# Two wave loads of the recurrence requested ahead of images 1 to 3

## The chip, the cores and the metric

The kernel runs on one core of one Trainium2 chip. The metric is the device time of one execution in microseconds (us), as the median of several runs. Profiles come from one further execution, which is recorded by the hardware profiler.

## The reference

Four images of 56 x 56 pixels with 128 channels pass through four layers:

- a neighbourhood attention (7 x 7 windows, four heads) with an MLP behind it,
- a recurrence of 16 steps with gates (three matrix products per pixel), whose complex coefficients come from Fourier transforms of two 7 x 7 kernels per channel,
- a softmax attention over all pixels and a mixture of eight experts, of which each pixel uses two,
- an attention by distances and a layer of 64 experts that choose their tokens.

What the change touches belongs to the second layer's coefficients:

```
A_f = fft2(pad(A_real + 1j * A_imag))        # 64 channels, 56 x 56
Ar, Ai = A_f.real, A_f.imag
mag = sqrt(Ar ** 2 + Ai ** 2 + 1e-08)
scale = 0.95 * sigmoid(mag) / (mag + 1e-08)
Ar, Ai = Ar * scale, Ai * scale              # and B_f without a scale
for _ in range(16):
    h_r, h_i = (fg_r * (Ar * h_r - Ai * h_i) + inp_r,
                fg_i * (Ar * h_i + Ai * h_r) + inp_i)
```

## The kernel before

The images stay in SBUF from start to end as `x[0]` to `x[3]`, 112 partitions (two image rows) by 28 tiles by 128 channels, and each layer adds its result to them. The first layer runs over 28 stripes of eight image rows, seven per image. `PERIOD` is a list, written by hand, of the steps of one round with their lags: round `i` computes the scores of stripe `i+1`, the sums of stripe `i`, the MLP of stripes `i-1` and `i-2`, and so on. The order of the instructions on TensorE, VectorE and ScalarE is exactly this order (`tc.manual_schedule`). Each of these engines works in order, so an instruction that waits holds up all behind it.

**The recurrence's transforms.** `Recurrence.transforms` works out the Fourier transforms as matrix products with a table of cosines and sines (`waves`, 113 rows: cosines in rows 0 to 48, sines in rows 64 to 112). It cuts the 1568 columns of half an image into eight portions of n = 196 columns. A portion is four steps: `products` (L1070: eight products with `taps` into two `f_ps`, copies into `fa` and `fb`, squares), `squared`, `magnitudes` and `scaled`. They are laid into the rounds of the first layer by `WAVES_AT`, one portion for each round, from round 1 on; `products` stands in each round behind the sums of the stripe (L713, L719).

Each `products` begins with the request of its part of the waves (L1073), 113 partitions by 2 by 196 numbers of 4 bytes. The part goes into two rows of `parts`, 0 and 1 for even portions, 4 and 5 for odd ones (`places`), so the request for portion 2 waits until TensorE is through with portion 0.

**The requests.** All DMA requests of this stretch are made by SyncE, in the order of the program text. In `neighbourhood_of_safe_scores` this order is: the bands and weights of the first layer; stripes 3 to 6 of image 0; then, from `transforms`, `taps` (113 rows), `gates_w`, `gates_b`, `group` and `late` (L1042 to L1046); then images 1 to 3, one request of 1568 KB each (L158); and then, as the rounds reach them, the eight parts of the waves:

```
        env.fetch(0, range(3, NG))
        plan = work(ps1, NG + 1)
        for b in range(1, B):
            env.fetch(b)
```

`work` is what calls `transforms`. The rounds come after these lines, and with them the requests of L1073.

**Who reads images 1 to 3 first.** The step `ahead` (L560, `bn_stats` on VectorE) takes the statistics of coming stripes. The step "statistics" calls it up to three times in each round, and it starts out ahead: stripes 7 and 8, the first two of image 1, come in round 0. Behind them on VectorE stand, in round 0, the copy of `b_vT` (L813) and the late constants of the projection, for which TensorE waits at L817, then the quotient (L727 to L732) and the bands (L675). Image 2 is first read in round 3.

Of the kernel before, what the change touches and what calls it, by code (L numbers as in the profile page):

```python
# [32 lines left out]
WAVES = 64 + K7 * K7  # L33
# [96 lines left out]
class Env:  # L130
# [41 lines left out]
    def load(self, pool, name, src):  # L172
        t = pool.tile(list(src.shape), F32, tag=name, name=name)
        self.nc.sync.dma_start(t, src)
        return t
# [826 lines left out]
class Recurrence:  # L1002
# [35 lines left out]
    def transforms(self, psum):  # L1038


        nc, ins, n = self.env.nc, self.env.ins, HALF // 8
        nc.sync.dma_start(self.taps, ins["taps"])  # L1042
        nc.sync.dma_start(self.gates_w, ins["gates_w"])
        nc.sync.dma_start(self.gates_b, ins["gates_b"])
        nc.sync.dma_start(self.group, ins["groups"])
        nc.sync.dma_start(self.late, ins["L0_conv_b_fc2"].unsqueeze(1))  # L1046

        def constants():
            nc.vector.tensor_scalar(
                self.gates_b[:, 0, :], self.gates_b[:, 0, :], 2.0, 0.5, ALU.add, ALU.mult  # L1050
            )
            nc.vector.tensor_scalar(
                self.gates_b[:, 1, :], self.gates_b[:, 1, :], 0.5, None, ALU.mult
            )
            nc.vector.tensor_scalar(self.group, self.group, 1.0 / (TOK * GC), None, ALU.mult)
            nc.vector.tensor_scalar(
                self.taps[64:WAVES, :, 1, :], self.taps[64:WAVES, :, 1, :], -1.0, None, ALU.mult
            )
            if not self.is_late:
                nc.vector.memset(self.late, 0.0)  # L1060
                nc.vector.memset(self.gates_b[:, 3, :], 0.0)

        def places(c0):

            at = 4 * (c0 // n % 2)
            return self.parts[:WAVES, at : at + 2, :n], *(
                self.parts[:, at + i, :n] for i in (2, 3)
            )

        def products(c0):  # L1070
            cols = slice(c0, c0 + n)
            waves, mag, _ = places(c0)
            nc.sync.dma_start(  # L1073
                waves, ins["waves"].rearrange("w (k t) -> w k t", k=2)[:, :, cols]
            )
            for i, out in enumerate((self.fa[:, 0:2], self.fb)):
                f_ps = psum.tile([128, 2, n], F32, tag="one", name="f_ps")
                for j in range(2):
                    for k, side in enumerate(self.SIDES):
                        nc.tensor.matmul(  # L1080
                            f_ps[side, j, :], self.taps[:, i, j, :], waves[:, k, :],
                            start=True, stop=True,
                        )
                nc.scalar.copy(out[:, :, cols], f_ps)
            nc.scalar.activation(self.fa2[:, cols], self.fa[:, 0, cols], AF.Square)
            nc.scalar.activation(mag, self.fa[:, 1, cols], AF.Square)

        def squared(c0):
            fa2, mag = self.fa2[:, c0 : c0 + n], places(c0)[1]
            nc.vector.tensor_tensor(fa2, fa2, mag, ALU.add)  # L1090


        def magnitudes(c0):
            fa2 = self.fa2[:, c0 : c0 + n]
            _, mag, gain = places(c0)
            nc.scalar.activation(mag, fa2, AF.Sqrt, bias=self.tiny)
            nc.scalar.activation(gain, mag, AF.Tanh, scale=0.5)

        def scaled(c0):
            fa, fa2 = self.fa[:, 0:2, c0 : c0 + n], self.fa2[:, c0 : c0 + n]  # L1100
            _, mag, gain = places(c0)
            nc.vector.tensor_scalar(mag, mag, 1e-8, 2.0 / 0.95, ALU.add, ALU.mult)
            nc.vector.reciprocal(mag, mag)
            nc.vector.scalar_tensor_tensor(gain, gain, 1.0, mag, ALU.add, ALU.mult)
            nc.vector.tensor_tensor(
                fa, fa, gain.unsqueeze(1).to_broadcast([128, 2, n]), ALU.mult
            )
            nc.vector.tensor_tensor(gain, gain, gain, ALU.mult)
            nc.vector.tensor_tensor(fa2, fa2, gain, ALU.mult)

        return constants, [
            [lambda c0=c0, step=step: step(c0) for step in (products, squared, magnitudes, scaled)]
            for c0 in range(0, HALF, n)
        ]
# [495 lines left out]
class Paced:  # L1610
# [6 lines left out]
    def step(self, share):  # L1617

        begun = set()
        while self.at < len(self.pieces):  # L1620
            piece = self.pieces[self.at]
            if share < 1 and (
                self.due[self.at] > self.total * share
                or getattr(piece, "apart", False) and getattr(piece, "list", None) in begun
            ):
                return
            piece()
            begun.add(getattr(piece, "list", None))
            self.at += 1
# [1386 lines left out]
```

## Time and profile before

| | us |
|---|---|
| median of 3 runs (lowest, highest) | 2504.63 (2502.03, 2505.33) |
| the profiled execution's own time | 2503.91 |
| its span, first to last instruction | 2502.0 |
| TensorE busy | 2386.4 (95%) |
| VectorE busy | 1841.4 (74%) |
| ScalarE busy | 1552.2 (62%) |
| GpSimd busy | 211.4 (8%) |

The span is shorter than the execution by what lies around the first and the last instruction. In the profile PE is TensorE's products and PEld its loading of weights, DVE is VectorE, ACT ScalarE, POOL GpSimd, SPq SyncE's queue of requests. A row of 40 digits cuts the span into slices of 62.6 us; the digit is the busy share in tenths. The mean clock that TensorE was granted is 0.97 of full speed. Line numbers are those of the kernel before.

### The profile page before, as it was taken

Reading aid. Unit: us, or ns where it says so; the run is one execution under the profiler, and the core shown is the slowest. Engines: PE = TensorE matmul, PEld = TensorE weight load, DVE = VectorE, ACT = ScalarE, POOL = GpSimd, SP = SyncE. Lnnn points to the kernel's source line nnn. Section 1 sums busy time; section 2 is a strip of 40 time slices with the busy share of each in tenths; the row PEclk is TensorE's granted clock in tenths of the full one; section 3 lists DMA queues with packets and bytes.
Section 4 is the critical chain, followed back from the end, with each engine's and each line's share of the span. In section 5 each row is a group of like instructions: output and inputs, shape, how many; then the busy total and the mean of one; then the engine's idle time right before and its main releaser. Section 6 shows DMA issues by size and latency. Waiting matters only on the chain.

```text
span 2502.0 us, 39490 instructions
## 1 busy us (share of the span) xinstructions
PE 2386.4 (95%) x14685; PEld 1294.7 (52%) x14685; DVE 1841.4 (74%) x5062; ACT 1552.2 (62%) x3343; POOL 211.4 (8%) x473
## 2 busy tenths in 40 slices
PE   6999999999999999999999999999999999996795
PEld 4777777775455555555544444445444434442334
DVE  5556899983997959799598687745888567777563
ACT  3899889875666646666422556484554765844681
POOL 4323354320000000000000000000000000000000
PEclk9999999999999999999999999999999998997688
DMA  6000000000000000000000000000000000002266
GB/s 141 13 10 2 2 2 2 2 2 9 1 1 1 1 1 1 1 1 1 12 1 1 1 1 1 1 1 1 1 1 1 1 1 1 1 1 109 76 256 205
DMA packets 39917, 53.95 MB, mean 22 GB/s; under 512 B 4104, under 2 KB 35443, under 8 KB 35620
## 3 DMA queue, kind: packets, MB, share of 16 engines
q1 hardware_dynamic: 39716, 51.34, 6.4%
q8 instruction: 118, 1.93, 0.3%
q14 instruction: 83, 0.68, 0.1%
HBM read 44.78 MB, written 6.42 MB: 20 GB/s over the span
## 4 chain that ended last, share of the span: by engine, by line
PE 67%; DVE 6%; ACT 2%; DMA 1%; issue 1%; SPq 0%; DVEq 0%; ACTq 0%
PE s_ps L2027 20%; PE o_ps L2110 20%; PE y_ps L1557 7%; PE d_ps L1825 4%; PE xT_ps L207 3%; PE g_ps L1196 2%; PE p_ps L2307 1%; PE l_ps L2266 1%; PE y_ps L2051 1%; PE q_ps L1789 1%; PE z_ps L2003 1%; PE l_ps L1522 1%; PE h_ps L2376 1%; DMA lot<-in_L_ffn_lots 1%; DVE x L2459 1%; PE o_ps L2405 1%
## 5 line engine op out<-in xcount | busy, mean ns | idle before, releaser
L2034 ACT ACTIVATE e<-s_ps 128x448 f32<-128x448 f32 x688 | 367.8, 543 | 514.8 <-PE s_ps L2027 510.2
L2027 PE MATMUL s_ps<-zT,xnT 128*128 128x448 f32 (+1 forms) x1400 | 649.1, 554 | 0.6 <-ACT e L2034 0.6
L2110 PE MATMUL o_ps<-e,keep 128*128 128x448 f32 (+1 forms) x1376 | 646.1, 552 | 0.0
L2110 PEld LDWEIGHTS o_ps<-e,keep 128*128 128x128 f32 (+1 forms) x1376 | 241.3, 190 | 214.9 <-issue 213.8
L2027 PEld LDWEIGHTS s_ps<-zT,xnT 128*128 128x128 f32 (+1 forms) x1400 | 240.2, 188 | 212.8 <-issue 190.9
L1837 ACT ACTIVATE d_ps<-d_ps,half 128x448 f32<-128x448 f32 (+1 forms) x384 | 232.2, 606 | 118.3 <-PE d_ps L1825 116.2
L1831 DVE TENSOR_REDUCE found<-d_ps 128x1 f32<-128x448 f32 x316 | 190.9, 619 | 72.0 <-PE d_ps L1825 69.7
L1557 PE MATMUL y_ps<-experts,xnT 128*112 128x512 f32 x448 | 215.5, 604 | 2.0 <-ACT d_ps L1837 1.7
L1562 DVE TENSOR_TENSOR gated<-y_ps,gate 112x512 f32<-112x512 f32 x224 | 151.5, 687 | 37.6 <-PE y_ps L1557 35.3
L1567 DVE TENSOR_TENSOR gated<-gated 112x512 f32<-112x512 f32 (+1 forms) x336 | 152.4, 462 | 3.0
L1825 PE MATMUL d_ps<-q_near,k_near 32*128 32x448 bf16 (+1 forms) x700 | 138.3, 373 | 9.4 <-ACT d_ps L1837 4.0
L207 PE MATMUL xT_ps<-ident,xn 112*128 112x112 f32 x672 | 118.4, 281 | 24.9 <-ACT xn L1657 16.9
L207 PEld LDWEIGHTS xT_ps<-ident,xn 112*128 112x128 f32 x672 | 79.7, 145 | 100.7 <-ACT xn L1657 52.1
L1557 PEld LDWEIGHTS y_ps<-experts,xnT 128*112 128x112 f32 x448 | 76.2, 178 | 97.6 <-issue 60.4
L1825 PEld LDWEIGHTS <-k_near 32*128 32x128 bf16 (+1 forms) x700 | 33.4, 92 | 167.1 <-issue 154.3
L675 DVE TENSOR_TENSOR e<-e,band 112x1792 f32<-112x1792 f32 (+3 forms) x56 | 100.0, 1788 | 15.4 <-ACT e L668 15.4
L780 PE MATMUL f_ps<-w_fc,h 128*112 128x128 f32 x896 | 104.8, 274 | 1.9 <-ACT h L771 1.6
L1657 ACT ACTIVATE xn<-x,g_off,g_rs 112x128 f32<-112x128 f32 x224 | 94.1, 484 | 19.3 <-DVE g_off L1647 9.0
L780 PEld LDWEIGHTS f_ps<-w_fc,h 128*112 128x112 f32 x896 | 99.8, 177 | 5.2 <-ACT h L771 4.8
L766 PE MATMUL h_ps<-zT,w_fc 128*128 128x448 f32 x224 | 88.9, 540 | 0.6 <-ACT zT L760 0.6
L668 ACT ACTIVATE e<-s_ps 112x1792 f32<-112x1792 f32 (+3 forms) x56 | 82.7, 1477 | 7.0 <-PE s_ps L659 4.0
L1201 ACT ACTIVATE parts<-g_ps,gates_b 128x224 f32<-128x224 f32 x168 | 65.8, 449 | 21.3 <-PE g_ps L1196 15.4
(404 smaller groups left out, 3935.7 us busy)
## 6 DMA issues: line engine op xcount, KB each, us to landing
lot<-in_L_ffn_lots SPq DMA_DIRECT2D x32, 1024.0 KB
out_x<-x SPq DMA_DIRECT2D x28, 224.0 KB
x<-in_x SPq DMA_DIRECT2D x3, 1568.0 KB
x<-in_x SPq DMA_DIRECT2D x7, 224.0 KB
parts<-in_waves SPq DMA_DIRECT2D x8, 173.0 KB
out<-found SPq DMA_DIRECT2D x64, 2.0 KB
w_fc<-in_L_conv_w_fc SPq DMA_DIRECT2D x2, 256.0 KB
experts<-in_L_ffn_expert_w SPq DMA_DIRECT2D x1, 512.0 KB
```

Of the source, the lines that this page charges most:

```text
L207: self.nc.tensor.transpose(ps[:, j * P : (j + 1) * P], xn[:, j, :], self.ident[:P, :P])
L675: nc.vector.tensor_tensor(es, es, bands[stripes[i][1] == 0][:n].rearrange("p h r c -> p h (r c)").unsqueeze(2) .to_broadcast([n, NH, m, 8 ...
L780: nc.tensor.matmul(f_ps[:, j, :], h[:, k, j * P : (j + 1) * P], w_fc2[:, k, :], start=(k == 0), stop=(k == 3),)
L1557: nc.tensor.matmul(y_ps, held["xnT"][g][:, j * P : (j + 1) * P], self.experts[:, 4 * i : 4 * i + 4, :], start=True, stop=True,)
L1562: nc.vector.tensor_tensor(gated[:, some, :], y_ps, gate[:, some].unsqueeze(2).to_broadcast([P, 4, C]), ALU.mult,)
L1567: nc.vector.tensor_tensor(gated[:, :n, :], gated[:, :n, :], gated[:, n : 2 * n, :], ALU.add)
L1825: nc.tensor.matmul(d, held["k"][part, 128 * c : 128 * c + n], held["q"][g][part, :], start=True, stop=True,)
L1831: nc.vector.tensor_reduce(self.found[:, self.most : self.most + 1], d, AX.X, ALU.max)
L1837: nc.scalar.activation(d, d, AF.Relu, bias=self.half[:n], accum_out=self.found[:n, self.sums : self.sums + 1],)
L2027: nc.tensor.matmul(s_ps[i * n : (i + 1) * n, :GW], self.xnT[:, at : at + n], zT, start=True, stop=True,)
L2034: nc.scalar.activation(e[:n], s_ps[:n, :GW], AF.Exp)
L2110: nc.tensor.matmul(sums[:, :GW], self.keep[:n, k, :], e[:n], start=(k == 0 and g - 1 not in pairs), stop=last,)
```

## The change

The function that asks for a part of the waves becomes a function of its own, `load`. `transforms` calls it for portions 0 and 1 right behind its other five requests, and `products` calls it for the other six only. As `transforms` runs before images 1 to 3 are requested, the two requests now stand ahead of those three in SyncE's queue. The places in `parts`, the sizes, and the order of the instructions on the other engines stay as they are.

```diff
         nc.sync.dma_start(self.late, ins["L0_conv_b_fc2"].unsqueeze(1))
 
+        def places(c0):
+
+            at = 4 * (c0 // n % 2)
+            return self.parts[:WAVES, at : at + 2, :n], *(
+                self.parts[:, at + i, :n] for i in (2, 3)
+            )
+
+        def load(c0):
+            nc.sync.dma_start(
+                places(c0)[0],
+                ins["waves"].rearrange("w (k t) -> w k t", k=2)[:, :, c0 : c0 + n],
+            )
+
+        early = range(0, 2 * n, n)
+        for c0 in early:
+            load(c0)
+
         def constants():
...
         def products(c0):
             cols = slice(c0, c0 + n)
             waves, mag, _ = places(c0)
-            nc.sync.dma_start(
-                waves, ins["waves"].rearrange("w (k t) -> w k t", k=2)[:, :, cols]
-            )
+            if c0 not in early:
+                load(c0)
```

## The prediction

> **What bounds the kernel now.** First the page, for which engine sets the time and where its row has holes; then who TensorE waits for in the first 85 us; then what the request queue and the DMA engines do there.
>
> ```profile
> PE 2386.4 (95%) x14685; PEld 1294.7 (52%) x14685; DVE 1841.4 (74%) x5062; ACT 1552.2 (62%) x3343; POOL 211.4 (8%) x473
> ...
> PE   6999999999999999999999999999999999996795
> ...
> x<-in_x SPq DMA_DIRECT2D x3, 1568.0 KB
> ...
> parts<-in_waves SPq DMA_DIRECT2D x8, 173.0 KB
> ```
>
> TensorE is busy for 95%, and its row is full from the second slice on. Between 85 and 122 us the waits name none of TensorE, so what is lost or won before about 85 us reaches the end unchanged. The first slice (6) is the only place that this change can touch. Who waits there (in total, times, longest):
>
> ```profile
> PE f_ps L1080 <- DMA parts<-in_waves: 5.4, 1, 5.4
> ...
> DVE st_all L560 <- DMA x<-in_x: 5.0, 1, 5.0
> ...
> PE bp_ps L817 <- DVE b_vT L813: 1.3, 1, 1.3
> ```
>
> Two DMA waits, not one: TensorE waits 5.4 us for wave load 0, and before that VectorE waits 5.0 us for image 1, with TensorE behind it. The order in time, from the timelines of SyncE, VectorE and TensorE (start, us, instruction, count, idle before it):
>
> ```profile
> 28.64 16.21 SPq L158 DMA_DIRECT2D x<-in_x  x3
> 44.90 21.90 SPq L1073 DMA_DIRECT2D parts<-in_waves  x3
> ...
> 42.88 1.65 DVE L560 BATCH_NORM_STATS2 st_all<-x 112x6 f32<-112x128 f32 x8 [4.98 <-DMA x<-in_x]
> 44.44 0.15 DVE L813 COPY b_vT<-bv_ps 128x1 f32<-128x1 f32 x1
> ...
> 44.64 0.46 PE L817 MATMUL bp_ps<-w_proj,b_vT 128*96 128x128 f32 x2 [1.32 <-DVE b_vT L813]
> ...
> 63.26 2.88 PE L1080 MATMUL f_ps<-parts,taps 113*64 113x196 f32 x16 [5.37 <-DMA parts<-in_waves]
> 66.07 3.33 PE L641 MATMUL v_ps<-w_qkv,xnT 128*112 128x128 f32 x14
> ...
> 84.69 1.55 PE L1080 MATMUL f_ps<-parts,taps 113*64 113x196 f32 x16
> 86.17 1.78 PE L641 MATMUL v_ps<-w_qkv,xnT 128*112 128x128 f32 x14
> ```
>
> Image 1 releases VectorE at 42.88; TensorE is ready for the first products at 63.26 − 5.37 = 57.9 and gets load 0 at 63.26. Last, what the DMA engines moved in these stretches (length, then busy us of PE, PEld, DVE, ACT, POOL, clock, DMA share, GB/s):
>
> ```profile
> 28.90:36.70 7.80, 6.14 (x72) 3.23 (x70) 3.16 (x2) 4.84 (x6) 7.25 (x18) 1.00 0.99 216
> 36.70:37.30 0.60, 0.60 (x29) 0.55 (x32) 0.60 (x3) 0.44 (x1) 0.60 (x1) 1.00 0.19 37
> ...
> 52.60:54.60 2.00, 2.00 (x5) 0.71 (x4) 1.94 (x6) 0.00 (x0) 0.00 (x0) 0.50 0.11 28
> 54.60:62.60 8.00, 3.29 (x113) 3.08 (x112) 5.49 (x21) 0.72 (x2) 2.52 (x9) 0.92 0.07 22
> ...
> 45.60:55.80 10.20, 9.44 (x73) 6.30 (x77) 9.76 (x25) 3.15 (x5) 0.20 (x2) 0.50 0.76 166
> ...
> 63.20:69.40 6.20, 6.14 (x34) 4.99 (x34) 0.36 (x1) 2.08 (x5) 0.00 (x0) 0.50 0.08 25
> ```
>
> These rows decide the case. An image uses all 16 DMA engines (share 0.99). A wave load uses one: share 0.07 is 1/16, and 22 GB/s for 8.0 us is 176 KB, one load of 113 x 2 x 196 x 4 B = 177 KB. So **a wave load is small, but holds one DMA engine for 8.0 us**. And that engine is one that the images use: in 52.6 to 54.6 a single engine finishes image 3 while the rest stand still, and load 0, long requested, starts only then. `taps`, also 113 rows, shows what such a load does to what comes behind it: it is requested ahead of the images, and the 1.6 MB of image 1 have passed by 36.7 (216 GB/s for 7.8 us is 1.7 MB), yet VectorE gets image 1 only at 42.88. The rest came late through one engine.
>
> **The change part by part.** Instructions and their order on TensorE, VectorE, ScalarE and GpSimd are the same in both kernels. On SyncE's queue two requests (0 and 1) of the eight at L1073 move past three, images 1 to 3. They write places in `parts` that nobody uses before, so no wait for an earlier reader comes with them. Images 2 and 3 now take over DMA semaphores last used by `taps` and the gate weights, which have landed long before; no cost.
>
> *Taken away:* TensorE's wait for load 0, 5.4 us. Load 0 would land near 43, load 1 near 51, both before 57.9. The next loads (2 and 3) are requested behind products 0 and 1 as before and have a period of 18.5 us (84.69 to 103.19); no cost.
>
> *The two issues themselves:* 2 x 0.63 us on SyncE (its usual time for one), beside all engines; the DMA engine is the longer price, so nothing is added for them.
>
> *Added:* image 1's share on that one engine stands behind two loads, 2 x 8.0 = 16.0 us. So does its release of VectorE: 42.88 becomes about 58.9. Two rules of the Trainium skill pull apart here. For the change speaks "DMA: Bandwidth & Descriptors", section "Rules for kernel authors": issue a DMA early and wait on it late. With only 346 KB more to pass at 216 GB/s it would make image 1 late by 1.6 us, and the sum would be negative. Against it speaks the same page's "Queues, rings and completion order": each DMA engine consumes its ring in order, and a transfer has landed only when every engine it uses has reported. Then the 16.0 us are due in full. The row of 52.60 to 54.60 is on the second rule's side, so I take 16.0. Lower bound: image 1's share of that engine is 98 KB, 4.6 us alone at 22 GB/s; by the trace's landing records the last small load ahead of it there landed at 34.70, so it used 8.2 us beside the other engines. Saving all of that gives 12.4. Upper bound: loads that run beside images are slower. At 216/16 = 13.5 GB/s each would take 13 us, 26 together; but in 36.70 to 37.30 the other engines soon stand still when one lags, so I go to 18 at most. Image 2 is first read near 101 us and image 3 later; image 3's last landing record stands at 55.1, so 16 us late both are still there by 71.2.
>
> *Who stands behind that wait:* VectorE is in order, so the `b_vT` copy, the projection's constants, the transposes and the bands wait with it; TensorE, also in order, stands at bp_ps, and ScalarE behind TensorE. From 42.88 to 54.1 VectorE has no gap, so nothing in that stretch takes up a delay. TensorE comes to the first products at 57.9 + 16.0 = 73.9, which is 10.6 us after 63.26.
>
> *Given back by the clock.* After today's 4.7 us hole the clock is at 0.50 (63.20 to 69.40). If TensorE comes to the products without a hole, that stretch runs as the next period does: products 2.88 to 1.55, values 3.33 to 1.78, queries 1.67 to 0.92, the 24 scores 1.48 to 0.86, transposes 0.89 to 0.60, in all 4.5 us. ScalarE, 9.15 busy of 10 us in 80 to 90, would then be late for the next products' copies by an estimated 0.5 us; I count 4.0. Today the clock is back at 1.00 by 55.8, 11.2 us after the restart at 44.64; a restart near 60.7 would have it back by 71.9, ahead of 73.9. The skill's "TensorE: Matmul & The Clock Gate", section "Part 1: The HAM clock gate", speaks against the change here: an idle window drops the clock to half, so a 16 us stall buys a new slow start, worth up to half of the 10.2 us that follow. But the row of 45.60 to 55.80 is already at 0.50 today and led by VectorE (9.76 of 10.20 busy), so I charge nothing more. Bounds for the clock's part: −4.5 to +1.
>
> Sum: 16.0 − 5.4 − 4.0 = **+6.6 us**. On the profiled execution's 2503.9 (span 2502.0 and 1.9 around it) this is 2510.5; the median of the runs stands 0.7 higher, so 2511.2.
>
> **The rivals.**
>
> *Forecast, 0.60:* as above; with a delay of 14 to 17.5, +4 to +8.5.
>
> *The clock does not come back, 0.16:* the longer stall leaves TensorE at half speed through the first products too. Then 16.0 − 5.4 = +10.6: 2515.2. For it: 11.2 us of slow restart in today's trace. Against: 2 us of margin in the sum above.
>
> *One load's worth, 0.14:* the two loads overlap, or the engine's share of image 1 gets through between them. Delay 8 to 12, sum −1.4 to +2.6: no change that can be measured. Against: 54.6 to 70.6 shows two loads one after the other at 22 to 24 GB/s.
>
> *Faster, 0.10:* the images do not stand behind the loads, because the moved loads use an engine whose image share is not the last to land. Image 1 is late by 1.6 us, 1.6 − 5.4 − 4.0 = −7.8: 2496.8. It decides when the delay is under 5.4 + 4.0 = 9.4 us. For it: TensorE's wait is real and the bytes few. Against: today's 42.88, six us after image 1's bytes had passed.
>
> **How the numbers follow.** A measurement of this kernel can tell about 0.2%, 5.0 us, from no change. The forecast case lies mostly above +5.0: of its 0.60 I put 0.48 in slower and 0.12 in same; with 0.16 for the slow clock and a little of the third case, slower has 0.65. Same has 0.25, faster 0.10. The range, 2505.5 to 2516, holds the forecast, the slow clock and the upper end of the third case; the faster case is left out.
>
> **What would show it right or wrong in the profile after.** VectorE's wait for the image at L560 near 58 to 59 us, some 21 us long instead of 5.0. TensorE's wait for `b_vT` 17 us instead of 1.3. No wait for the wave loads at L1080, first products near 74, second near 91.3 (84.69 + 6.6). A DMA share of 0.07 for much of 29 to 47. The clock at 1.00 through the first products. I am wrong if VectorE gets image 1 before 52 us, or if the second products start within 2 us of 84.69.

## The result and the profile after

| | before | changed |
|---|---|---|
| median of 20 runs each, us | 2504.57 | 2510.42 |
| profiled execution, us (its span) | 2503.91 (2502.0) | 2512.44 (2510.6) |
| first products at L1080 / L1089, us | 63.26 | 73.06 |
| second products, us | 84.69 | 93.18 |
| from there to the end of the span, us | 2417.3 | 2417.4 |

The ratio of the runs is 1.0024 (95% interval 1.0017 to 1.0031): slower by 5.9 us, between 4.3 and 7.8. One of the 20 runs of the changed kernel took 4767.54 us in a slow state that no profile shows; the ratio leaves it out, and without it the median is 2510.20. In the changed kernel the lines behind `transforms` have moved by 9 (L1080 is L1089, the requests of L1073 are L1056). The last row of the table says that in these two profiled executions whatever differs lies before the second products; the 2417 us behind them are the same. That they agree so closely is in part chance: in the other eleven profiles of this document the same stretch takes 2415.0 to 2422.5 us. So times are compared by the medians of the runs, and the profiles serve for the first 95 us.

Who waits between 42 and 75 us in the changed kernel, from its waits (in total, times, longest):

```profile
...
DVE st_all L560 <- DMA x<-in_x: 19.0, 1, 19.0
ACT xnT L603 <- PE xT_ps L207: 16.2, 1, 16.2
...
PE bp_ps L817 <- DVE b_vT L813: 15.3, 1, 15.3
```

TensorE's wait for the wave loads is gone from this list. VectorE's wait for image 1 has grown from 5.0 to 19.0 us, TensorE's wait behind it from 1.3 to 15.3. The times, from the timelines of SyncE, VectorE and TensorE:

```profile
28.23 8.51 SPq L1056 DMA_DIRECT2D parts<-in_waves  x2
36.79 23.93 SPq L158 DMA_DIRECT2D x<-in_x  x3
...
58.43 1.65 DVE L560 BATCH_NORM_STATS2 st_all<-x 112x6 f32<-112x128 f32 x8 [18.97 <-DMA x<-in_x]
60.00 0.14 DVE L813 COPY b_vT<-bv_ps 128x1 f32<-128x1 f32 x1
...
60.19 0.74 PE L817 MATMUL bp_ps<-w_proj,b_vT 128*96 128x128 f32 x2 [15.31 <-DVE b_vT L813]
...
73.06 1.55 PE L1089 MATMUL f_ps<-parts,taps 113*64 113x196 f32 x16
74.54 1.78 PE L641 MATMUL v_ps<-w_qkv,xnT 128*112 128x128 f32 x14
...
79.51 1.02 PE L622 MATMUL q_ps<-xnT,w_qkv 128*128 128x448 f32 x2 [1.67 <-ACT xnT L603]
...
93.18 1.55 PE L1089 MATMUL f_ps<-parts,taps 113*64 113x196 f32 x16
```

Image 1 now releases VectorE at 58.43, 15.6 us later than before. What the DMA engines did meanwhile (columns: length, busy us of PE, PEld, DVE, ACT, POOL, clock, DMA share, GB/s):

```profile
28.90:36.70 7.80, 6.14 (x80) 4.50 (x79) 2.02 (x1) 5.48 (x8) 7.34 (x21) 1.00 0.08 25
36.70:44.00 7.30, 7.30 (x165) 5.63 (x165) 2.34 (x5) 2.37 (x6) 6.50 (x20) 1.00 0.08 24
44.00:48.00 4.00, 0.87 (x8) 0.69 (x7) 0.00 (x0) 1.47 (x1) 1.37 (x3) 0.82 0.71 179
48.00:52.00 4.00, 0.00 (x0) 0.00 (x0) 0.00 (x0) 0.00 (x0) 0.00 (x0) 0.50 1.17 226
...
73.00:79.50 6.50, 4.84 (x74) 3.91 (x66) 3.58 (x11) 4.69 (x9) 2.96 (x7) 1.00 0.04 13
80.80:87.40 6.60, 6.60 (x44) 5.10 (x37) 3.14 (x6) 5.87 (x8) 0.67 (x1) 0.50 0.04 12
```

From 28.90 to 44.00 little more than one engine of sixteen works (0.08; one is 0.06). Before, 216 GB/s of image 1 moved in the first of these rows. The images did not only lose their share on the one engine: by the packet records none of their parts started before 45, when load 1 was well under way (41.3 to 50.2). The last two rows are the clock: full through the first products, then half for nearly 7 us.

### The profile page after: what moved, and what is told of

Same layout as the page of the kernel before. It is cut to its first block, busy times and chain, and to the rows that moved or that the text cites. A ratio compares the mean times of both kernels' runs of the same rounds, so it can differ in the third digit from the quotient of the medians.

```text
span 2510.6 us, 39486 instructions
## 1 busy us (share of the span) xinstructions
PE 2384.3 (95%) x14685; PEld 1294.6 (52%) x14685; DVE 1840.9 (73%) x5062; ACT 1552.0 (62%) x3343; POOL 211.2 (8%) x473
## 4 chain that ended last, share of the span: by engine, by line
## 5 line engine op out<-in xcount | busy, mean ns | idle before, releaser
L1834 PE MATMUL d_ps<-q_near,k_near 32*128 32x448 bf16 (+1 forms) x700 | 137.6, 369 | 10.2 <-ACT d_ps L1846 4.3
```

The source lines that it names most:

```text
L1834: nc.tensor.matmul(d, held["k"][part, 128 * c : 128 * c + n], held["q"][g][part, :], start=True, stop=True,)
```

## The experiments

All times are medians against the runs of the kernel before that were made with them (2504.57 to 2505.56 us). The column "released" is when image 1 releases VectorE in the profile (a line of L560 with a DMA wait in front of it; "no wait" where there is none).

| run | released | first products | second products | time, us | ratio (95% interval) |
|---|---|---|---|---|---|
| changed, again | 57.37 | 71.99 | 92.11 | +5.1 | 1.0019 (1.0011 to 1.0026) |
| load 0 alone early | 49.25 | 63.74 | 83.83 | −1.6 | 0.9990 (0.9981 to 0.9999) |
| loads behind image 1 | 39.98 | 53.79 | 73.94 | −11.4 | 0.9957 (0.9944 to 0.9971) |
| early, on 16 engines | 43.26 | 55.62 | 75.74 | −8.2 | 0.9967 (0.9955 to 0.9979) |
| image 1 read later | 58.25 | 53.92 | 70.88 | −9.6 | 0.9964 (0.9950 to 0.9977) |
| taps on 16 engines | no wait | 57.70 | 74.65 | −9.5 | 0.9959 (0.9946 to 0.9973) |
| early loads and taps on 16 | 40.05 | 53.80 | 73.94 | −9.1 | 0.9963 (0.9950 to 0.9975) |
| loads behind image 1, hole filled | 40.00 | 55.73 | 73.14 | −11.4 | 0.9951 (0.9937 to 0.9966) |
| all on 16, nothing moved | no wait | 55.99 | 76.13 | −10.8 | 0.9951 (0.9938 to 0.9965) |
| the same, hole filled | no wait | 55.77 | 73.19 | −14.6 | 0.9936 (0.9922 to 0.9950) |
| changed, hole filled | 56.81 | 71.27 | 88.69 | +1.3 | 1.0006 (0.9998 to 1.0015) |

**One load instead of two.**

```diff
-        early = range(0, 2 * n, n)
+        early = range(0, n, n)
```

> Only load 0 stands ahead of images 1 to 3; load 1 is requested with its products. Theory (a load of 113 rows holds one DMA engine for 8 us, and image 1's share on that engine queues behind it): image 1 releases VectorE one load earlier than with two, near 58.4 - 7.9 = 50.5 us; first products near 65, second between 82 and 85.3; the time within -2.6 to +0.6 us of the kernel before. Rival (any request ahead of the images makes SyncE's queue hand them on late, whatever engines it uses): about as late as with two loads, near 58. Rival (the images are late only by the bytes ahead of them): near 43.7, first products near 59, time -5 to -8 us.

VectorE's line for image 1 in this run:

```profile
49.25 1.64 DVE L560 BATCH_NORM_STATS2 st_all<-x 112x6 f32<-112x128 f32 x8 [9.40 <-DMA x<-in_x]
```

One load less, 8.1 to 9.2 us earlier (57.37 and 58.43 in the two profiles of the changed kernel). Both rivals (58 or 43.7) are out. The gain and the loss nearly cancel: −1.6 us. So the delay goes by the load, and a break-even lies between one load and two.

**The loads between image 1 and image 2.**

```diff
         for b in range(1, B):
             env.fetch(b)
+            if b == 1:
+                work.requests()
```

`work.requests` calls `load` for the two early portions; the lines that take these calls out of `transforms` and hand them on are left out here.

> Loads 0 and 1 are requested between image 1 and image 2. Theory: image 1 releases VectorE at 42.9 as in the kernel before, the loads take the one engine from there on and land near 51 and 59, images 2 and 3 are 16 us late, which nobody meets before about 100 us. First products near 57.9 without a hole, second near 75 (clock at full speed throughout) to 78; time -6.5 to -10 us. Rival (the move costs because the two loads and the images share bandwidth, or because of the two issues themselves): no better than the changed kernel, +6 us. Rival (the first products wait for something else once the loads are there): no gain against the kernel before.

VectorE and TensorE in this run:

```profile
39.98 1.64 DVE L560 BATCH_NORM_STATS2 st_all<-x 112x6 f32<-112x128 f32 x8 [2.40 <-DMA x<-in_x]
...
53.79 1.55 PE L1090 MATMUL f_ps<-parts,taps 113*64 113x196 f32 x16
```

At the first products this is 4.1 us better than expected (57.9). Image 1 releases VectorE 2.9 us sooner than in the kernel before: its late share took 5.8 us and not 8.2 by the landing records, probably because no other image runs beside it. TensorE is at bp_ps 1.4 us sooner (43.25), and from there to the first products it takes 10.5 instead of 13.3 us: in the kernel before the clock was at half for some 10 us of that way (45.60 to 55.80), here only from 44.8 to 48.2. TensorE's wait for the loads is gone as in the changed kernel, and so is the stall. The idea of the change was sound; image 1 is what the two loads must not stand in front of.

**The same place, but sixteen engines.**

```diff
-            nc.sync.dma_start(
-                places(c0)[0],
-                ins["waves"].rearrange("w (k t) -> w k t", k=2)[:, :, c0 : c0 + n],
-            )
+            src = ins["waves"].rearrange("w (k t) -> w k t", k=2)[:, :, c0 : c0 + n]
+            for rows in (slice(0, 112), slice(112, WAVES)) if c0 in early else (slice(0, WAVES),):
+                nc.sync.dma_start(places(c0)[0][rows], src[rows])
```

> As the changed kernel, but each of the two early loads is requested as 112 rows and 1 row, so that it spreads over 16 DMA engines. Same bytes, same place in the queue, two requests more. Theory (the one engine is the price): image 1 is late by about 1.5 us only, VectorE released near 44; first products near 59, second between 76 and 79; time -5.5 to -8.5 us. Rival (bytes or requests ahead of the images are the price): VectorE released near 58 as in the changed kernel, time +6 us or more.

```profile
43.26 1.64 DVE L560 BATCH_NORM_STATS2 st_all<-x 112x6 f32<-112x128 f32 x8 [3.89 <-DMA x<-in_x]
```

The same bytes in the same place, with two requests more, take the delay away: 43.26 against 58.43, and −8.2 us against +5.9. The one engine, and so the number of rows, 113, was the price; the bytes and the place were not. The Trainium skill has the rule for it ("DMA: Bandwidth & Descriptors", section "Why a DMA increments its semaphore by 16 and not by 1"): a transfer runs on the largest number of engines up to 16 that divides the slowest dimension of both sides. 112 gives 16, the prime 113 gives 1. This case agrees: the share is 0.07 to 0.08 with 113 rows, and by the landing records the request of 112 rows reports from 16 engines, that of 113 rows from one.

**Image 1 read one round later.** The transfers are those of the changed kernel:

```diff
-                "statistics": lambda i: ahead_to(i + NG + 3),
+                "statistics": lambda i: ahead_to(NG - 1 if i <= 1 else i + NG + 3),
```

> As the changed kernel, but VectorE reads image 1 one round later: its statistics for stripes 7 and 8 move from round 0 into round 1 (three stripes in each of the next rounds). Nothing is done to the transfers. Theory (the price is VectorE's in-order wait, with TensorE behind it): image 1 still lands near 58.4, but the wait at it is short and falls behind TensorE's work of round 0 and 1; no wait of TensorE for b_vT, first products near 57, second between 74 and 77.5; time -7 to -10.5 us. Rival (late transfers cost by themselves, through contention or through images 2 and 3): still slower than the kernel before.

VectorE and TensorE in this run:

```profile
58.25 2.42 DVE L560 BATCH_NORM_STATS2 st_all<-x 112x6 f32<-112x128 f32 x12 [3.81 <-DMA x<-in_x]
...
53.92 1.55 PE L1089 MATMUL f_ps<-parts,taps 113*64 113x196 f32 x16
...
70.88 1.55 PE L1089 MATMUL f_ps<-parts,taps 113*64 113x196 f32 x16
```

Image 1 lands at 58.25, as late as in the changed kernel, and it costs nothing that can be told: the wait falls to 3.8 us and stands behind what TensorE needs. So it was not the lateness, but the place of the first reader in VectorE's order. (The first products come 3 us sooner than expected, with the same short spell of half clock as with the loads behind image 1.)

**taps on sixteen engines, nothing else.**

```diff
-        nc.sync.dma_start(self.taps, ins["taps"])
+        for rows in (slice(0, 112), slice(112, WAVES)):
+            nc.sync.dma_start(self.taps[rows], ins["taps"][rows])
```

> The kernel before, with only the request of taps (113 rows, the other load on one engine, ahead of image 1) made as 112 rows and 1 row. Theory (what stands on that engine ahead of image 1 sets when VectorE gets it; the next thing late then sets the end): image 1 releases VectorE near 38 instead of 42.9 and TensorE's wait for b_vT is gone, so TensorE is ready for the first products near 53 to 54; but load 0 still stands behind image 3 on that engine and lands near 61 to 62, so TensorE's wait there grows from 5.4 to about 8 us. First products near 61.5, time -1 to -2 us: not to be told from no change. Rival (VectorE's wait for image 1 is worth its 5 us): -5 us.

This missed widely: −9.5 us instead of −1 to −2. VectorE's wait went, as expected, but TensorE's wait at the first products fell too, to 1.9 us (the profile puts it down to "issue"; load 0's landing record, 57.6 against a start at 57.70, says that it was the load). The windows of this run say why:

```profile
28.90:36.70 7.80, 6.13 (x80) 4.49 (x79) 2.02 (x1) 5.40 (x8) 7.34 (x21) 1.00 1.12 246
36.70:37.30 0.60, 0.60 (x3) 0.08 (x1) 0.10 (x1) 0.46 (x1) 0.50 (x3) 1.00 1.16 281
37.30:42.90 5.60, 5.60 (x133) 4.55 (x136) 3.77 (x13) 1.34 (x4) 5.22 (x12) 1.00 1.20 234
```

The row of 36.70 to 37.30, where the kernel before had 0.19 and 37 GB/s, is full. With one engine lagging, the others had stood still between two images; without, the three images follow each other and the last landing record of them is at 50.7 instead of 55.1. Load 0 lands at 57.6 instead of 63.1. I had counted what taps cost image 1 and not what the lag cost images 2 and 3. That is 5.6 us of the 10.0 by which this profile is ahead at the second products; the other 4.5 are the clock, which stayed at full speed from the first products to the second (17.0 us against 21.4). In how many executions it does so is not shown. The kernel before had the same trouble as the changed one, in small: a load of 113 rows ahead of image 1.

**Both on sixteen engines.** The diffs of the last two runs on sixteen engines together.

> As the run with the early loads on 16 engines, and taps on 16 engines too. Theory: nothing holds the one engine ahead of image 1 any more; VectorE gets it near 39 to 40, no wait worth naming on VectorE or TensorE up to the products; first products near 53 to 54, second near 73.5 with a spell of half clock or 70.5 without; time -8 to -12 us, some 2 us better than the loads alone on 16 engines (VectorE released near 43.3 there). Rival (the rest of the gain there was held back by something else than image 1): no better than that run, -8.2 us.

No gain over the loads alone on sixteen engines that can be told (−9.1 and −8.2 us). VectorE is released 3.2 us sooner (40.05 and 43.26), but TensorE waits no longer than 0.3 us for `b_vT` in either: 43.26 was soon enough. That the first products come 1.8 us sooner in this profile was decided before any of it: TensorE is at the `b_vT` transpose 1.8 us sooner too (the copy behind it at 43.05 and 44.89), as the clock stayed at full speed from 32.5 to 35.9, where it was at half with the loads alone on sixteen engines. All versions without a stall have their first products at 53.8 to 53.9 or at 55.6 to 56.0, by where the clock was at half before them: at the start, or, in the run with the loads behind image 1 and the hole filled (below), for 6.8 instead of 3.4 us ahead of the products. The table is to be read with that.

**All on sixteen engines, nothing moved.** taps as above, and all eight loads at their old place:

```diff
-            nc.sync.dma_start(
-                waves, ins["waves"].rearrange("w (k t) -> w k t", k=2)[:, :, cols]
-            )
+            src = ins["waves"].rearrange("w (k t) -> w k t", k=2)[:, :, cols]
+            for rows in (slice(0, 112), slice(112, WAVES)):
+                nc.sync.dma_start(waves[rows], src[rows])
```

> The kernel before with nothing moved: taps and all eight wave loads are requested where they were, each as 112 rows and 1 row. Theory (the price and the wait both came from loads on one engine, not from their place in the queue): the images land by about 51 us as in the run with taps alone on 16 engines, load 0 within 2 us of them, so neither VectorE nor TensorE waits for a DMA; first products near 55.8 instead of 57.7 there, time about 11 us below the kernel before, 2 us below the run with taps alone. Rival (the loads must be asked for early to be there in time): TensorE still waits at the first products, -9.5 us as with taps alone.

```profile
55.99 1.55 PE L1081 MATMUL f_ps<-parts,taps 113*64 113x196 f32 x16
```

No wait for a DMA is left between 36 and 100 us on either engine, and the first products come at 55.99. The loads need not be asked for earlier at all; −10.8 us, not to be told from the best move (−11.4). Against taps alone (−9.5) the medians don't separate.

**The hole of round 1 filled.** TensorE waits 1.67 us for ScalarE's copy ahead of the queries of round 1, in all versions. Seven small products go into it. They write an unused corner of the transposes' place in PSUM (`fill[0]`; the lines that set it are left out), so the copy comes behind them and a wait of 0.62 us remains:

```diff
             ps = env.transposed(ps1, held[i]["xn"])
+            if i == 4:
+                for _ in range(7):
+                    nc.tensor.matmul(
+                        fill[0][:, 448:512], env.ident, env.ones[:, :64], start=True, stop=True,
+                    )
```

First with the loads between the images, then with all loads on sixteen engines, then in the changed kernel, with the changed kernel itself beside it:

> As the run with loads 0 and 1 between images 1 and 2, and in round 1 seven products of ones with the identity, whose result nobody reads, fill the 1.67 us in which TensorE waits for ScalarE's copy ahead of the queries. Work is only added. Theory (this hole is what drops TensorE's clock to half for 6.8 us behind the first products, which is why the changed kernel's profile got back 1.3 us there and not 4.0): first to second products 17 us as in the run that read image 1 later, not 20.1; the clock at 1.00 between them; time 2 to 4 us below the run with loads 0 and 1 between the images. Rival (the drop has another cause, such as the pause ahead of round 1, or the load on TensorE): 20.1 us again, time as there or slower by the added work, 0 to +1 us.

> As the run before it in this list, with the seven products of ones and the identity that nobody reads in TensorE's 1.67 us wait of round 1. Theory (the hole drops the clock in most executions): first to second products 17 to 17.5 us, no half clock between them; median 1 to 2 us below the same kernel without them. Rival (the earlier gain of 0.7 us was chance): no difference.

> The changed kernel with the same seven products in the hole of round 1. Theory: the stall of 15 us for image 1 and its 58.4 stay, first products near 73, but the second come 17 to 17.5 us behind them and not 20.1, as the clock stays at 1.00: the time is then some 3 us below the changed kernel in those executions in which its clock dropped. Rival (after so long a stall the clock drops again anyway): 20.1 us.

> The changed kernel once more, on the same chip and in the same rounds as the one with the filled hole, for the comparison and for a second profile. Theory: VectorE gets image 1 near 58.4 again, first products near 73; first to second products either 17 us (clock at full speed) or 20 us (6.8 us at half), and the time +5 to +8.5 us accordingly.

TensorE and the windows in the changed kernel with the hole filled:

```profile
71.27 1.55 PE L1098 MATMUL f_ps<-parts,taps 113*64 113x196 f32 x16
...
75.89 1.69 PE L609 MATMUL xT_ps<-ones,ident 128*128 128x64 f32 x14
78.19 1.02 PE L631 MATMUL q_ps<-xnT,w_qkv 128*128 128x448 f32 x2 [0.62 <-ACT xnT L612]
...
88.69 1.55 PE L1098 MATMUL f_ps<-parts,taps 113*64 113x196 f32 x16
...
80.00:87.40 7.40, 7.40 (x87) 5.03 (x91) 4.57 (x14) 7.33 (x11) 2.32 (x9) 1.00 0.04 10
```

The clock stays at 1.00 where it fell to 0.50 before, and from first to second products it is 17.4 us; the changed kernel has 20.1 in both of its profiles. The queries themselves come 0.5 us later than without the added products (6.92 us behind the first products and not 6.45), so the gain is the clock's and not that of an earlier start. The median falls by 3.8 us with the added work, from 2510.64 to 2506.83 (1.0019 to 1.0006; the intervals share no more than 1.0011 to 1.0015). With all loads on sixteen engines it falls by 3.8 too (2494.76 to 2490.92), but there the intervals overlap widely. In the first of the three, 17.4 us stand against 20.2, but the medians differ by 0.7 us only (2493.17 and 2493.87, from different sets of runs): the expected 2 to 4 us did not show. In its profile 1.9 us of the gain were lost ahead of the first products (55.73 against 53.79), mostly in the longer spell of half clock named above; whether that is so in the other executions is not known. All three profiles with the hole filled have no drop; of the nine others that were made of kernels with any change, seven have 20.1 to 20.2 us and two (taps alone, image 1 read later) 17.0. So the hole is what drops the clock, in most executions and not in all.

The clock records of these traces say more on when. In the first 100 us the clock changes only in steps of 3.4 us (spells of half clock of 3.4, 6.8, 10.2, 13.7 and 23.9 us), so each trace can be cut into such steps. These are the step with the hole and the next one, first in the changed kernel and then with taps alone on sixteen engines:

```profile
77.28:80.70 3.42, 1.75 (x18) 0.89 (x18) 1.63 (x1) 3.33 (x6) 2.75 (x4) 1.00 0.07 23
80.70:84.11 3.41, 3.41 (x33) 2.73 (x30) 1.42 (x2) 3.15 (x5) 0.77 (x1) 0.50 0.07 23
...
60.41:63.82 3.41, 2.07 (x42) 1.62 (x40) 0.68 (x3) 2.80 (x4) 1.23 (x3) 1.00 0.07 22
63.83:67.24 3.41, 3.09 (x35) 2.11 (x36) 1.95 (x1) 3.41 (x7) 2.27 (x2) 1.00 0.07 22
```

In eight of the ten profiles without added products (the kernel before among them) the whole hole lies in one step, TensorE is busy for 0.51 of it, and the clock falls at its end. With taps alone two steps share the hole (0.61 and 0.91) and it does not fall. With image 1 read later the hole begins within 0.05 us of the edge of a step, nearer than modelled ends can tell, and it does not fall. With the added products the share is 0.82. So whether this hole costs anything seems to go by where it falls among these steps. The share alone is not the rule: ahead of the first products the clock fell behind a step of 0.74 (44.75, loads behind image 1). Where the limit lies is not shown.

The lowest median is that of the version with everything on sixteen engines and the hole filled: 2490.92 us, 0.9936 of the kernel before; the gain of the filled hole in it is not clear of noise. Without work for its own sake, the versions at 2493.87 (loads behind image 1) and 2494.76 (sixteen engines, nothing moved) beat both kernels and don't differ measurably.

## Why the prediction was right, point by point

It said 2511.2 and was 0.8 us above the median.

*The 5.4 us taken away:* right. No wait for the loads is left at L1089; the landing records have load 0 at 41.3 and load 1 at 50.2.

*16.0 us added:* 15.6 in the profile, 14.5 in the second one. The two loads took 7.6 and 8.9 us, 16.5 together; the small load ahead of them landed 1.0 sooner than before (33.7 and 34.7), and image 1's share on the engine took 8.2 behind them, what it took before. One load instead of two leaves 6.4 of it, sixteen engines take it away but for 0.4: this shows the order on one engine, and that of the two rules the one of "Queues, rings and completion order" was the one to follow here. (That a transfer has landed only when every engine that it uses has reported stands on the same page in "Why a DMA increments its semaphore by 16 and not by 1"; here image 1's other parts had reported by 53.7, and VectorE was released by the last one at 58.4.) The working missed that images 1 to 3 would not start on the other fifteen engines either (0.08 from 28.90 to 44.00); for image 1 this changed nothing, as the one engine was last anyway.

*VectorE and TensorE stand behind it:* right, and shown by reading image 1 later. TensorE came to the first products at 73.06 instead of 73.9. Its wait was 15.3 and not 17 because it reached the place 1.6 us later than before: at the start, around 26 us, the clock came up a little later in this execution (two query products 1.70 instead of 0.92 us). This was absorbed by the stall.

*No charge for a new slow start:* right. From bp_ps to the products it is 12.9 us in the changed kernel (60.19 to 73.06) and was 13.3 (44.64 to 57.89).

*4.0 us given back by the clock:* **the term that was mis-sized.** The profile gave back 1.3 (21.4 us from first to second products became 20.1), the second profile the same. The first products did run at full speed, 1.55 instead of 2.88 us. But the 1.67 us hole behind the scores then dropped the clock for 6.8 us, which the runs with the hole filled show (3.8 us by the medians in the changed kernel). The profile before held the warning: after its own hole near 71 to 72.6 the clock was at 0.50 a second time, until 76.3, and I counted the end of that spell as gain instead of asking whether it would come again.

*The sum:* by the profiled executions it is +8.5 (15.6 and some tenths less on the way, −5.4, −1.3), 1.9 above the +6.6. By the medians it is +5.9. The two profiled executions lie on opposite sides of their medians, the changed one 2.0 above, the one before 0.7 below, which makes up the difference of 2.6. In how many executions of the changed kernel the clock fell, and so how much of the 4.0 came back in the median, is not shown: profiles exist of two only. The forecast's nearness to the median is in part luck.

*The rivals:* the faster one needed a delay under 9.4 us; the delay was 15.6. "One load's worth" needed 8 to 12 and did not come true either: the two loads followed each other. Where one load alone was moved, the delay was 6.4 us (42.88 to 49.25), and the time −1.6. The slow clock did not come at the first products; it came only behind them.

## What to carry to other kernels

Look at how many DMA engines a transfer uses before moving it: a share of 0.07 beside a low rate is one engine, and a request of 113 rows, small in bytes, may hold up everything behind it that uses that engine too. Splitting such requests (here into 112 rows and 1) was worth as much as the best order of requests (−10.8 and −11.4 us), and it needs no thought about what stands behind them. And when a wait is removed by asking earlier, name who is now asked later and what is its first reader: here the long early load was free only where nothing waited in order behind what it displaced.

## What the runs showed of the hardware

- While one engine lagged, the others did not run ahead into the next transfers: 24 to 25 GB/s for 15 us in the changed kernel, with 4.7 MB of images still to come, and 37 GB/s for 0.6 us in the kernel before between images 1 and 2. With no one-engine request in front, the same transfers ran at 234 to 281 GB/s without a gap. SyncE stood at its requests meanwhile: 8.51 us for those of the two loads, where one usually takes 0.63, and then 7.7 us (from 36.79) for that of image 1. So the images were held back at their requests too, and not on the one engine alone.
- A hole of 1.67 us in an otherwise full TensorE was enough to halve its clock for 6.8 us, at a price of some 3 us, in seven of the nine profiles of changed versions without added products. In all seven the hole lay in one of the 3.4 us steps in which the clock changes; in the one profile where two steps clearly shared it, the clock stayed up.
